# Planned transfer times, ranks and tile counts in a depthwise-attention and selective-scan kernel

## The chip, the cores and the metric

The kernel runs on one core of a Trainium2 chip. Its time is device microseconds of one execution. Five engines take part: TensorE (PE in the profile; its weight loads are listed apart as PEld), VectorE (DVE), ScalarE (ACT), GpSimd (POOL), and SyncE (SP), which here only issues transfers. Each engine runs its own list of instructions in order; semaphores hold an instruction back until what it needs is there.

## The reference

x has 8 images of 56 x 56 positions and 192 channels. Two layers follow each other, both added to x. The first is an attention whose queries and keys come from depthwise 3 x 3 convolutions. The second is a selective scan in four directions. Cut to what matters here:

```python
x = x + conv_attention(group_norm(x))            # layer 0
xz = einsum('bhwc,oc->bhwo', group_norm(x), in_proj_w);  xa, z = split(xz)
xc = silu(depthwise_conv3x3(xa) + conv_b)        # 384 channels
xs = four orders of xc: rows, columns, and both reversed      # L = 3136 positions
dts, Bs, Cs = split(einsum('bkdl,kcd->bkcl', xs, x_proj_weight))
delta = softplus(dt_projs(dts) + dt_projs_bias)
for l in range(L):                               # per direction, 384 channels x 16 states
    h = exp(delta[l] * A) * h + delta[l] * Bs[l] * xs[l]
    y[l] = sum over the 16 states of h * Cs[l]
y = sum of the four directions back in place + xs * Ds
out = x + out_proj(layer_norm(y) * silu(z))
```

## The kernel before, in words

All is done in fp32. The *front* of an image (norms, convolutions, attention, projections; `front` and `x_proj`) writes its results to DRAM. The *scan* then goes through 224 chunks: 8 images x 4 directions x 7 chunks of T = 448 positions. In a chunk the 384 channels lie as 3 blocks (j) of 128 partitions, and there are 16 states n. So there are 3584 pairs (chunk i, state n). The front of the next image and the finish of the last one are done during the scan.

For one chunk, `prepared` loads three tiles (dts, the row inputs of delta; ct, the factors C; du, the scan's input xs), computes delta into dl by a chain PE (L1066), ACT (L1069, L1071), DVE (L1073), ACT (L1078), DVE (L1081), ACT (L1083), DVE (L1085), three times, and lets POOL multiply du by dl (L1089). Then for each n:

- `row_loads` loads row n of B, spread over 128 partitions, into a tile bb (224 KB; a ring of 3 tiles). For the states that POOL sums it also loads the row of C into cb.
- `inputs_made`: POOL makes h = du x bb (L1126; 128 x 1344). The tiles h form a ring of HBUFS = 8.
- `decays`: ACT makes da = exp(dl x A) in PSUM, 3 instructions (L1140), two banks.
- `scans`: DVE scans h in place, 3 instructions (L1157). `carries` keeps the last column (L1179).
- For 11 of the 16 states (13 in the last image), `turned` transposes h on PE (L1203), `scaled` multiplies by C on ACT (L1219), and `back` transposes into the PSUM tile y, summing there (L1237).
- For the other states, `by_pool` multiplies h by cb on POOL (L1256) and adds to yp, one tile (L1260); `summed` adds yp to y on PE (L1275).

When a chunk's y is complete, `evicted` adds it to yacc on DVE (L1290, L1292). `skips` loads xs into yacc before the first direction.

The order in which all this stands on the engines is made by a planner in the kernel itself, `Sched`, when the program is built. Every piece of work is a generator that yields (engine, cost, cells read, cells written). The planner keeps its own clock for each engine, with fixed costs (`t_act`, `t_dve`, `t_pool`). Each time it takes the piece with the least `t - rank`, where t is when the piece could start: a larger rank goes earlier. A transfer yields SP, a cost of 0.07 and a fifth number, the time until its data are there. Cells (`Cell`) hold the planned times of the last write and the last read; a piece cannot start before the cells that it reads are written and those that it writes are no longer read. Ring tiles are given out when they are free in the plan.

`pace` holds the front within 12 us of PE time of a target; when it falls behind, its rank becomes URGENT. `ending` does so for the finish. Where the plan leaves PE idle for over 0.45 us, warm-up matmuls on zeros fill the gap (`keep_busy`, L1371).

The plan decides only the order. On the chip the semaphores decide the time: a planned wait is not executed, but what stands later in an engine's list cannot pass what stands earlier. SP's list is one queue for all transfers: a load that waits for its tile holds all later ones back.

Of the kernel before, what the change touches and what calls it, by code (L numbers as in the profile page):

```python
# [21 lines left out]
T = 448  # L22
# [14 lines left out]
R = 12  # L37
# [4 lines left out]
BY_POOL = (((2, 7), (12,)), ((2, 5), (8, 10), (13,)))  # L42
EPS = 1e-5
CAP = 60.0
HBUFS = 8
LEAD = 3


# [5 lines left out]
PE, ACT, DVE, POOL, SP = range(5)  # L54
LATE = (0.17, 0.08, 0.09, 0.06, 0.0)
HOP = 0.04
URGENT = 0.4


FILL = 64  # L60
# [103 lines left out]
class Sched:  # L164
# [37 lines left out]
    def give(self, s, t):  # L202

        e, cost, reads, writes = s.req[:4]
        end = t + cost
        self.at[e] = end
        self.used[e] += cost
        if s.group is not None and e == PE:
            self.spent[s.group] = self.spent.get(s.group, 0.0) + cost
        end = t + s.req[4] if len(s.req) > 4 else end + LATE[e]  # L210
        for c in reads:
            c.r = max(c.r, end)
        for c in writes:
            c.w = end
        s.end = max(s.end, end)
        self.resume(s)

    def run(self, until=None):
        while True:
# [20 lines left out]
            for s in self.stages:  # L240
# [3 lines left out]
                if s.group in self.limit:  # L244
# [4 lines left out]
                    if spent < must:  # L249
                        rank = URGENT  # L250
                e, _, reads, writes = s.req[:4]
# [21 lines left out]
def kernel(  # L273
# [93 lines left out]
    for nm, src in (("q", bn_q), ("kv", bn_kv)):  # L367
        p = load(f"bn{nm}", [CP, 4, NB], src.rearrange("v (b p) -> p v b", p=CP))
        s = const.tile([CP, NB], F32, name=f"bns{nm}")
        t = const.tile([CP, NB], F32, name=f"bnt{nm}")  # L370
# [30 lines left out]
    s3 = Rings(ctx.enter_context(tc.tile_pool(name="s3", bufs=3)), 3)  # L401
    sh = Rings(ctx.enter_context(tc.tile_pool(name="sh", bufs=HBUFS)), HBUFS)
    c1 = Rings(ctx.enter_context(tc.tile_pool(name="c1", bufs=1)), 1)
# [3 lines left out]
    sc = Sched()  # L407
# [57 lines left out]
    def dma(reads, writes, late, dst, src, after=()):  # L465
        yield SP, 0.07, reads, writes, late
        nc.sync.dma_start(dst, src)
        for t in after:
            t.free()
# [563 lines left out]
    for i in range(2):  # L1033
        t = keep.tile([128, T], F32, name=f"dts{i}")
# [70 lines left out]
    def row_loads():  # L1105
        for i, n in todo:
            b, k, c, _ = steps[i]
            yield lambda: i in chunks
            m = made[b]
            cols = slice(c * T, (c + 1) * T)  # L1110
            bb = yield s3("bb", [128, T])
            yield from dma([m["k_rows"][k, c]], bb.c, 3.2, bb.ap, m["rows"][k][R + n, cols].partition_broadcast(128))
            brow[i, n] = bb
            if n in by[i]:
                cbr = yield s2("cb", [128, T])
                yield from dma([m["k_rows"][k, c]], cbr.c, 3.2, cbr.ap,
                               m["rows"][k][R + NST + n, cols].partition_broadcast(128))
                crow[i, n] = cbr
# [178 lines left out]
    with tc.manual_schedule():  # L1297
        order = [(lay, c) for lay in range(2) for c in range(NCH)]

        with tc.tile_pool(name="p8", bufs=8, space=PSUM) as p8:  # L1300
            banks[0] = Ring(lambda: p8.tile([128, 512], F32, name="bank0"), 8)
            sc.spawn(front(0), 0.0, "front")
            sc.run()
            main = sc.spent.pop("front")
            sc.spawn(x_proj(0, order[:LEAD]), 0.0, "front")
            sc.run()
            each = sc.spent.pop("front") / LEAD

        with ExitStack() as es:
            py = es.enter_context(tc.tile_pool(name="py", bufs=1, space=PSUM))  # L1310
            pa = es.enter_context(tc.tile_pool(name="pa", bufs=2, space=PSUM))
            pb = [es.enter_context(tc.tile_pool(name=f"pb{i}", bufs=1, space=PSUM)) for i in range(3)]
            ybanks = py.tile([128, NJ, 512], F32, name="y")
            nc.vector.memset(ybanks, 0.0)
            ry = Ring(lambda: ybanks, 1)
            rda = Ring(lambda: pa.tile([128, 512], F32, name="da"), 2)
            three = [Tile(1) for _ in pb]

            def share(name, most):
                return Share(three, [lambda p=p: p.tile([128, 512], F32, name=name, tag="bank") for p in pb], most)  # L1320

            rht, rprep = share("ht", 2), share("prep", 1)
            banks[0] = share("bank1", 1)
            at["chunk"] = 0

            for rank, g in enumerate((prepared, skips, row_loads, inputs_made, decays, scans, carries, turned, scaled,
                                      by_pool, back, summed, evicted)):
                sc.spawn(g(), 0.3 + 0.01 * rank, "scan")

            per = NDIR * NCH * NST  # L1330

            def ended(b):
                first = b * NDIR * NCH + (NDIR - 1) * NCH
                yield lambda: at["chunk"] >= first
                yield from finish(b, lambda c: lambda: at["chunk"] >= first + NCH - c, yread[b])

            def arounds():
                for b in range(nb):
                    yread[b] = {}
                    sc.spawn(ended(b), 0.0, "finish")  # L1340
                    if b > 0:
                        yield lambda: at["chunk"] >= b * NDIR * NCH
                    else:
                        yield from sc.join([sc.spawn(x_proj(0, order[LEAD:]), 0.0, "front")])
                    if b + 1 < nb:
                        yield from sc.join([sc.spawn(front(b + 1), 0.0, "front")])
                        yield from sc.join([sc.spawn(x_proj(b + 1, order), 0.0, "front")])

            def pace():

                b, slot = divmod(at["scan"], per)
                whole = main + len(order) * each
                lead = each * (len(order) - LEAD)
                before = b * whole + (lead if b else 0.0)
                here = whole + (0.0 if b else lead)
                late, share = (NDIR - 1) * NCH * NST, 0.87
                part = share * slot / late if slot < late else share + (1.0 - share) * (slot - late) / (per - 2 * NST - late)
                want = before + here * part
                return want + 12.0, want - 12.0

            def ending():
                done = sum(len(r) for r in yread.values())
                b, c = divmod(at["chunk"], NDIR * NCH)
                come = b * NCH + max(c - (NDIR - 1) * NCH, 0)
                return 1e9, 1e9 if done < come - 1 or done < b * NCH else 0.0

            def warm():

                while True:
                    yield PE, T_FILL, [], []  # L1370
                    nc.tensor.matmul(ybanks[:, 0, T:T + FILL], zeros, zeros[:, :FILL], start=False, stop=False)  # L1371

            def may():
                y = ys.get(at["y"])
                return y is not None and y["left"][0] > 0 and y["on"]

            at["y"] = -1
            filler = Stage(warm(), 0.0, 0.0, None)
            sc.resume(filler)
            sc.filler = filler, may  # L1380
            sc.limit["front"] = pace
            sc.limit["finish"] = ending
            sc.spawn(arounds(), 0.0)
            sc.run()
# [58 lines left out]
```

## Time and profile before

| | |
|---|---|
| median of 3 runs | 18865.54 us (18856.12 to 18895.47) |
| the profiled execution | 18891.11 us, span 18889.4 us |
| mean granted clock of TensorE | 0.971 |
| DVE, ACT busy | 14534.5 us, 14643.6 us |
| POOL busy | 16416.5 us |
| PE busy, of it L1371 | 16973.1 us, 1651.3 us |
| DMA | 1750.79 MB, mean 93 GB/s, 32.2% of 16 engines' span |
| L1157 DVE scans | 9216 of mean 1136 ns, 1536 of mean 1077 ns |
| L1126 POOL h | 3584, mean 3050 ns |
| L1089 POOL du | 224, mean 3047 ns |

The profile is of one execution. A row of a group gives busy time, the mean of one instruction and the engine's idle time just before them, with what ended it. A row of waits gives the engine and line that waited, what released it, the total in us, how often, and the longest. In a row in order of time, start and length stand first, and the idle time before it and its releaser in brackets.

### The profile page before, as it was taken

The numbers are of one execution on the slowest core, as the hardware profiler recorded it, in microseconds if no ns is written. First come the engines' busy times: TensorE is split into PE (matmuls) and PEld (weight loads), VectorE is DVE, ScalarE is ACT, GpSimd is POOL, SyncE is SP. The second block draws the span as 40 slices with busy tenths as digits, with TensorE's granted clock in tenths as the row PEclk, the third lists the DMA queues.
The fourth block names the chain that finished last, engine by engine and source line by source line (L and its number), as shares of the span: only waits on it lengthen the run. The fifth ranks groups of instructions, "written<-read, shape, count | busy, mean of one in ns | idle before, by whom it ended". The sixth has DMA issues, their size and how long they took to land. (4 is left out here: it accounts for less than half of the span.)

```text
span 18889.4 us, 274433 instructions
## 1 busy us (share of the span) xinstructions
PE 16973.1 (90%) x96640; PEld 11599.8 (61%) x96640; DVE 14534.5 (77%) x19156; ACT 14643.6 (78%) x26598; POOL 16416.5 (87%) x7528
## 2 busy tenths in 40 slices
PE   8789998999889998899898998889988899988888
PEld 4465566666666656665666655666556665666776
DVE  2387877887778777787777877778777788778887
ACT  2378877787777878778787887878778788888888
POOL 0388998899989999899998999989999899999997
PEclk9899999999999999999999999999999999999999
DMA  1332334323333333322333333332333333342222
GB/s 52 111 89 82 96 96 120 82 85 92 104 112 84 83 95 104 112 84 81 105 100 107 83 84 101 104 106 83 83 96 110 100 83 86 100 120 76 78 78 64
DMA packets 1128347, 1750.79 MB, mean 93 GB/s; under 512 B 168516, under 2 KB 1110840, under 8 KB 1123896
## 3 DMA queue, kind: packets, MB, share of 16 engines
q1 hardware_dynamic: 1126968, 1733.23, 32.2%
q8 instruction: 764, 12.52, 0.3%
q14 instruction: 615, 5.04, 0.1%
HBM read 1545.05 MB, written 187.74 MB: 92 GB/s over the span
## 5 line engine op out<-in xcount | busy, mean ns | idle before, releaser
L1157 DVE TENSOR_TENSOR_SCAN h<-da,newc,h 128x448 f32<-128x448 f32 x9216 | 10111.4, 1136 | 2166.1 <-ACT da L1140 1155.7
L1126 POOL TENSOR_TENSOR h<-du_s,bb 128x1344 f32<-128x1344 f32 x3584 | 10836.0, 3050 | 280.5 <-DMA bb<-rows 246.0
L1140 ACT ACTIVATE da<-dl_s,acoef 128x448 f32<-128x448 f32 x10752 | 6762.2, 636 | 1149.4 <-DVE h L1157 968.0
L1219 ACT ACTIVATE g<-ht,ct_s 112x384 f32<-112x384 f32 x10080 | 5663.7, 576 | 1776.0 <-PE ht L1203 1701.2
L1237 PE MATMUL y<-ident,g 112*128 112x112 f32 x30240 | 4742.3, 271 | 660.2 <-ACT g L1219 506.3
L1237 PEld LDWEIGHTS y<-ident,g 112*128 112x128 f32 x30240 | 3305.9, 143 | 3236.8 <-ACT g L1219 2466.3
L1203 PE MATMUL ht<-ident,h 128*112 128x128 f32 x30240 | 4935.7, 277 | 287.4 <-DVE h L1157 87.4
L1203 PEld LDWEIGHTS ht<-ident,h 128*112 128x112 f32 x30240 | 3481.3, 135 | 1064.4 <-issue 450.9
L1256 POOL TENSOR_TENSOR yp<-h,cb 128x448 f32<-128x448 f32 x1932 | 2147.0, 1143 | 454.8 <-PE y L1275 216.6
L1157 DVE TENSOR_TENSOR_SCAN h<-da,h 128x448 f32<-128x448 f32 x1536 | 1598.9, 1077 | 406.0 <-ACT da L1140 214.3
L1089 POOL TENSOR_TENSOR du_s<-dl_s,du_s 128x1344 f32<-128x1344 f32 x224 | 682.6, 3047 | 1338.5 <-DVE dl_s L1085 1300.8
L1256 POOL TENSOR_TENSOR h<-h,cb 128x448 f32<-128x448 f32 x1260 | 1399.1, 1141 | 291.3 <-issue 175.6
L1371 PE MATMUL y<-zeros 128*128 128x64 f32 x11944 | 1651.3, 272 | 0.0
L1371 PEld LDWEIGHTS y<-zeros 128*128 128x128 f32 x11944 | 1586.1, 198 | 48.6 <-issue 48.6
L1275 PE MATMUL y<-yp,ident 128*128 128x448 f32 x3864 | 1594.0, 547 | 5.1 <-POOL yp L1260 4.5
L453 PE MATMUL bank<-xa,dg 128*128 128x440 f32 (+2 forms) x3024 | 1318.4, 543 | 89.0 <-ACT g L1219 52.2
L1260 POOL TENSOR_TENSOR yp<-yp,h 128x1344 f32<-128x1344 f32 x420 | 1280.9, 3050 | 1.6
L757 PE MATMUL bank<-qT,kT 128*112 128x448 f32 x2352 | 1101.8, 559 | 83.8 <-ACT pT L707 47.2
L766 PE MATMUL bank<-pT,vt 112*128 112x448 f32 x2352 | 1002.1, 546 | 66.8 <-ACT pT L707 43.4
L1275 PEld LDWEIGHTS y<-yp,ident 128*128 128x128 f32 x3864 | 701.3, 193 | 551.6 <-issue 505.2
L453 PE MATMUL bank<-band,dgq 96*96 96x440 f32 (+3 forms) x2016 | 860.9, 544 | 54.4 <-ACT hq L583 29.9
L707 ACT ACTIVATE pT<-bank,nsh 112x448 f32<-112x448 f32 x1176 | 744.3, 635 | 172.9 <-PE bank L757 152.5
(152 smaller groups left out, 12958.1 us busy)
## 6 DMA issues: line engine op xcount, KB each, us to landing
bb<-rows SPq DMA_DIRECT2D x3584, 224.0 KB
cb<-rows SPq DMA_DIRECT2D x1064, 224.0 KB
xt<-x1d SPq DMA_DIRECT2D x224, 336.0 KB
du_s<-xch SPq DMA_DIRECT2D x112, 672.0 KB
du_s<-xcw SPq DMA_DIRECT2D x112, 672.0 KB
xch<-xv SPq DMA_DIRECT2D x24, 1568.0 KB
xcw<-xw SPq DMA_DIRECT2D x168, 224.0 KB
xs<-xch SPq DMA_DIRECT2D x56, 672.0 KB
```

What stands on the lines that cost most here:

```text
L453: nc.tensor.matmul(out[:, o0:o1, a:b], lhs, img(lo, hi)[:, :, a + dx - 1:b + dx - 1], start=(t == TAPS[0]), stop=(t == TAPS[-1]))
L757: nc.tensor.matmul(ps.ap[:TP, :T], kts[h][:, kb * TP:(kb + 1) * TP], qh.ap, start=True, stop=True)
L1126: nc.gpsimd.tensor_tensor(h.ap, du.ap, bb.ap.unsqueeze(1).to_broadcast([128, NJ, T]), ALU.mult)
L1140: nc.scalar.activation(da.ap[:, :T], dl.ap[:, j], AF.Exp, scale=acoef[:, k * NJ + j, n:n + 1])
L1157: nc.vector.tensor_tensor_scan(h.ap[:, j, rev], da.ap[:, 0:T][:, rev], h.ap[:, j, rev], news[i - 1].ap[:, j, n:n + 1] if ci else 0.0, ALU. ...
L1203: nc.tensor.transpose(ht.ap[:TP, j * 128:(j + 1) * 128], h.ap[:, j, s * TP:(s + 1) * TP], ident)
L1219: nc.scalar.activation(g.ap, ht.ap[:TP, :DIN], AF.Copy, scale=ct.ap[:, s, n:n + 1])
L1237: nc.tensor.matmul(y["t"].ap[:, j, s * TP:(s + 1) * TP], g.ap[:, j * 128:(j + 1) * 128], ident[:TP, :TP], is_transpose=True, start=(n == 0 ...
L1256: nc.gpsimd.tensor_tensor(to.ap[:, j], h.ap[:, j], cbr.ap, ALU.mult)
L1260: nc.gpsimd.tensor_tensor(yp.ap, yp.ap, h.ap, ALU.add)
L1275: nc.tensor.matmul(y["t"].ap[:, j, :T], ident, yp.ap[:, j], start=False, stop=(y["left"][j] == 0))
L1371: nc.tensor.matmul(ybanks[:, 0, T:T + FILL], zeros, zeros[:, :FILL], start=False, stop=False)
```

## The change

Five things change, all in what the planner is told. The transfers' planned times grow by MARGIN = 3 us. URGENT rises from 0.4 to 0.9. The ring of bb has 5 tiles, and a load of bb may be planned only AFTER = 2 us past the planned last use of its tile. The ring of h has 7 tiles. And the thirteen generators of the scan get ranks of their own, instead of 0.30 to 0.42 in steps of 0.01 in this order: `prepared` 0.30, `skips` 0.31, `row_loads` 0.32, `inputs_made` 0.33, `decays` 0.34, `scans` 0.35, `carries` 0.36, `turned` 0.37, `scaled` 0.38, `by_pool` 0.39, `back` 0.40, `summed` 0.41, `evicted` 0.42. A tile h takes 5376 bytes of a partition, a tile bb 1792.

```diff
-HBUFS = 8
+HBUFS = 7
...
-URGENT = 0.4
+MARGIN = 3.0
+AFTER = 2.0
+URGENT = 0.9
...
-        end = t + s.req[4] if len(s.req) > 4 else end + LATE[e]
+        end = t + s.req[4] + MARGIN if len(s.req) > 4 else end + LATE[e]
...
-            bb = yield s3("bb", [128, T])
-            yield from dma([m["k_rows"][k, c]], bb.c, 3.2, bb.ap, m["rows"][k][R + n, cols].partition_broadcast(128))
+            bb = yield s3("bb", [128, T], 5)
+            free = Cell()
+            free.w = bb.last() + AFTER
+            yield from dma([m["k_rows"][k, c], free], bb.c, 3.2, bb.ap, m["rows"][k][R + n, cols].partition_broadcast(128))
...
-            for rank, g in enumerate((prepared, skips, row_loads, inputs_made, decays, scans, carries, turned, scaled,
-                                      by_pool, back, summed, evicted)):
-                sc.spawn(g(), 0.3 + 0.01 * rank, "scan")
+            for g, rank in ((prepared, 0.3), (skips, 0.0), (row_loads, 0.25), (inputs_made, 0.0), (decays, 0.37),
+                            (scans, 0.16), (carries, 0.36), (turned, 0.37), (scaled, 0.38), (by_pool, 0.39),
+                            (back, 0.4), (summed, 0.0), (evicted, 0.71)):
+                sc.spawn(g(), rank, "scan")
```

## The prediction

> **What bounds the kernel now.** First the busy times of the page, then the whole kernel cut into start-up (front of batch 0), batches 0 to 6, and the last batch (columns: us, PE, PEld, DVE, ACT, POOL busy with counts, clock, DMA share, GB/s).
>
> ```profile
> PE 16973.1 (90%) x96640; PEld 11599.8 (61%) x96640; DVE 14534.5 (77%) x19156; ACT 14643.6 (78%) x26598; POOL 16416.5 (87%) x7528
> 0.00:786.60 786.60, 645.81 (x1906) 332.98 (x1906) 124.48 (x289) 204.02 (x319) 9.14 (x18) 0.92 0.23 71
> 786.60:16871.00 16084.40, 14559.60 (x82350) 9863.62 (x82351) 12706.36 (x16679) 12698.64 (x23050) 14590.75 (x6746) 0.97 0.34 96
> 16871.00:18889.40 2018.40, 1767.72 (x12386) 1403.21 (x12383) 1703.67 (x2189) 1740.94 (x3229) 1816.60 (x764) 0.96 0.27 78
> ```
>
> PE's 90% contains 1651.3 us of warm-up matmuls (L1371), so it really needs 81%. After start-up POOL is the fullest: 14590.75 of 16084.40 us, 91%, then 90%; DVE and ACT have 79% in the long stage. POOL idles 1494 + 202 us there. Next, who ends POOL's idle time, and SP's (us in total, times, longest):
>
> ```profile
> POOL du_s L1089 <- DVE dl_s L1085: 1300.8, 78, 729.9
> POOL h L1126 <- DMA bb<-rows: 246.0, 74, 9.7
> POOL yp L1256 <- PE y L1275: 216.6, 55, 12.9
> POOL h L1256 <- issue: 175.6, 55, 14.7
> POOL yp L1256 <- issue: 138.0, 75, 5.7
> SPq L467 <- POOL h L1126: 9514.5, 2843, 23.7
> ```
>
> Without the one start-up wait of 729.9 us the first row is 571 us; with what other releasers add, all idle time ahead of L1089 is 608 us after start-up. It is one repeated bubble, the hand-over between chunks. One of them, in order of time:
>
> ```profile
> 8446.12 0.62 DVE L1085 TENSOR_TENSOR dl_s<-prep,dl_s 128x448 f32<-128x448 f32 x1 [1.27 <-ACT prep L1083]
> 8446.82 3.04 POOL L1089 TENSOR_TENSOR du_s<-dl_s,du_s 128x1344 f32<-128x1344 f32 x1 [6.43 <-DVE dl_s L1085]
> 8449.94 9.06 POOL L1126 TENSOR_TENSOR h<-du_s,bb 128x1344 f32<-128x1344 f32 x3
> 8453.02 2.19 DVE L1157 TENSOR_TENSOR_SCAN h<-da,newc,h 128x448 f32<-128x448 f32 x2 [6.28 <-POOL h L1126]
> ```
>
> DVE finishes delta of the next chunk only when it has scanned everything of this one. POOL stands 6.43 us, then needs 3.04 us (du) and 3 us (first h), and DVE stands 6.28 us. I counted on each engine how many scans stand on DVE behind the last delta operation of the next chunk. At 89 of 223 boundaries it is none; there POOL's gap at L1089 averages 6.81 us (606 us, practically all of it). With one it is 0.07 us (33 boundaries), with two or more zero.
>
> **What the Trainium skill says.** "Perfetto Trace Analysis", Identifying the Most-Contended Engine and Optimization Strategy: occupancy is a fair measure for GpSimd, and the gaps on the fullest engine within a regime are what to trace. The numbers above are that reading, and agree. "DMA: Bandwidth & Descriptors", Queues, rings and completion order: on each DMA engine the descriptors of a ring are taken in order. The trace agrees: at 757 us a 21 KB load of dts stands behind seven 672 KB loads of yacc, and PE waits 17.64 us for it. "SBUF — State Buffer", Who interferes with whom: a DVE copy in a two-port mode and GpSimd block each other for a whole instruction. The trace agrees: the 96x2 copy of L430 has a median of 2.44 us and a longest of 9.20 us, beside unbroken POOL work.
>
> **The change, part by part.** No arithmetic is added or removed; the counts of the built programs are equal except warm-up matmuls. What moves is the order.
>
> Ranks. The multiply by inputs (inputs_made) falls from 0.33 to 0 and prepared stays at 0.30, scans fall from 0.35 to 0.16. In the old program L1089 stands directly ahead of its own chunk's first h in all 224 cases. In the new one it stands 2 to 10 h ahead in 223. On DVE, 3 to 13 scans of the old chunk (8 on average) remain when delta is done; none is left at a chunk boundary only for the first chunk. So the bubble goes. What can remain is POOL reaching the earlier du before delta: the h made ahead, less the scans that delta stands behind, is 0 in 7 cases, 1 in 47, more in 170. POOL was 2.1 h ahead of the scans on average, so the 47 may cost up to a scan set of 3 x 1.136 = 3.4 us, 160 us; by the old row 3 us. I take 50, and 7 x 6.81 = 50: 608 - 100 = **508 us gained** (bounds 400 and 608).
>
> bb from 3 to 5 tiles, 3 us margin on every transfer, 2 us behind the release. All are decisions of the planner; no instruction waits longer on the chip by itself. 3 tiles let bb be loaded while two h (6.1 us) are made, and the chain shows landings of 6.57 to 7.10 us; 5 tiles give four h, 12.2 us, less 2. Of the 246 us I keep 50: **196 gained** (bounds 100 and 246). SP's row of 9514.5 us tells that its queue stands on bb's release; behind it stand dts, ct, du and all loads of the front, now issued earlier relative to bb, which is also what feeds delta in time. At start-up the seven yacc loads (skips, rank 0) move behind dts, ct and du: **17 gained** of the 17.64 (0 to 20).
>
> h from 8 to 7 tiles. Nothing waits for an h tile now (1.5 us). With the release times of this trace, the seventh tile back would have been late at 178 h, by 561 us together; much of that would be eaten by slack, as POOL is ahead then. I take **100 lost** (0 to 561).
>
> summed at rank 0 and evicted at 0.71. On PE the sums of yp now stand 1.3 h behind the group's last turned h, against 1.8 ahead; the next write of yp stays 3 or more h away (6.6 on average, was 8.8). The row of 216.6 us can grow: **60 lost** (-50 to 217). Evicting first on DVE is 0.6 us each, hidden by the scans' wait for ACT (1369.9 us); nothing taken; the bound is the 90.5 us that DVE stands before its evictions now (L1290 and L1292), either way.
>
> Longer unbroken POOL runs hold DVE's port longer: DVE's excess over its medians is 160 us now; **40 lost** (0 to 160). URGENT 0.9 only reorders front work inside the same pace window; 0, hidden by the 19% that PE has over; without that cover the 0.5 us between the two ranks at each of 224 chunks, 112 either way. Warm-up matmuls grow from 5972 to 6468, two records each of 138 ns: 137 us of PE, only where the plan leaves PE idle; 0, at most 137.
>
> Sum: -508 - 196 - 17 + 100 + 60 + 40 = -521. The profiled execution, 18891.1 us (span 18889.4), becomes 18370; the median of the runs, 18865.5, stands 25.6 lower: **18345 us**, 2.8% faster.
>
> **Rivals.** (1) The gain goes into the ACT-DVE loop. DVE waits 1369.9 us for da and ACT 968.0 for the scan, with two da banks. Boundaries with one scan of lead have no POOL gap, but their chunks take 82.8 us against 84.4: 89 x 1.6 = 142, and a quarter of bb, 60: about 18665. Against it: three scans of lead have 74.0 us, though these chunks may carry less front work. (2) More goes: POOL's 741 us ahead of L1256 halve too, because by_pool now has 2.9 h made ahead, not 2.2. -608 - 246 - 370 - 17 + 150: about 17775. Against it: those gaps hardly depend on that number now (0.81, 0.72, 0.48, 1.15 us for 1 to 4). (3) Slower: the h ring binds. If POOL must be as far ahead as the earlier du makes it, each release counts as later: shifted by 3 us, 386 h are late by 1410 us together, and with half of it eaten by slack 18865 - 721 + 100 + 705 is 18949. It decides from 621 us on. Against it: 8 tiles were all alive at only 26 of 3584 h. (4) No effect: the orders slip against the real durations until the same bubble stands elsewhere; about 18865. Against it: a lead of 8 scans is 27 us.
>
> **Numbers.** My forecast (18,100 to 18,600) 0.52; rival 1 (18,600 to 18,820) 0.20; rival 2 (17,700 to 18,100) 0.12; rival 3 (18,905 to 19,300) 0.11; rival 4 (18,830 to 18,900) 0.05. The range leaves out rivals 3 and 4 and the lowest third of rival 2: 17,900 to 18,820. Faster or slower means by over 0.2%, about what a measurement of this kernel can tell from no change: 0.84 faster, 0.05 same, 0.11 slower.
>
> **What would show it.** Right: idle ahead of the du multiply after start-up near 100 us, the bb wait under 60, POOL at 93 to 94% of the middle stage, the first du near 769 us. Rival 1: those gone, but DVE's wait for da or ACT's for ht much longer. Rival 3: POOL's L1126 row ended by ht on PE, hundreds of us. Wrong altogether if POOL's idle time stays at 1.7 ms with new names.

## The result, and the profile after

The changed kernel takes 18710.28 us (median of 4 runs, 18697.01 to 18724.76). The kernel before, run beside it, takes 18874.99 us. The ratio is 0.9909, with an interval of 0.9895 to 0.9924: 0.9% faster, 165 us. The forecast was 2.8%, 521 us. So the direction was right and the time lies in the wide range (17,900 to 18,820), but less than a third of the gain came, and it lies outside the forecast's own range (18,100 to 18,600), in that of rival 1.

The profiled execution has a span of 18702.4 us. First the busy times of its page.

```profile
PE 17028.2 (91%) x97632; PEld 11660.0 (62%) x97632; DVE 14685.1 (79%) x19156; ACT 14645.0 (78%) x26598; POOL 16432.2 (88%) x7528
```

No engine works less. DVE is even 151 us busier, to which a section below returns. Next the same cut as before into images 0 to 6, with a front beside the scan, and the last image, without one (columns: us, busy PE, PEld, DVE, ACT, POOL with counts, clock, DMA share, GB/s).

```profile
785.00:16766.50 15981.50, 14620.35 (x82814) 9918.99 (x82814) 12832.52 (x16681) 12713.67 (x23056) 14603.79 (x6746) 0.98 0.34 96
...
16766.50:18702.40 1935.90, 1764.21 (x12909) 1409.86 (x12909) 1728.18 (x2187) 1727.15 (x3224) 1819.25 (x765) 0.99 0.28 80
```

The long stage became 102.90 us shorter (16084.40 before), and the last image 82.50 us (2018.40 before). That is the first finding: the last image, an eighth of the work, brought almost half of the gain. It gained 4.1%, each earlier image 0.6%. Whatever took the gain away sits where a front runs.

Now POOL's waits, and those of its queue of transfers (in us, times, longest).

```profile
POOL du_s L1091 <- DVE dl_s L1087: 881.2, 88, 728.1
POOL h L1260 <- issue: 318.5, 65, 13.9
POOL h L1260 <- DVE newc L1183: 272.9, 131, 12.1
POOL yp L1260 <- PE y L1279: 191.9, 95, 7.6
POOL h L1130 <- PE ht L1207: 190.2, 63, 9.1
POOL h L1130 <- DMA bb<-rows: 110.1, 30, 6.5
...
SPq L469 <- POOL h L1130: 4917.7, 1537, 14.4
SPq L469 <- POOL yp L1260: 3821.5, 419, 30.7
```

The prediction shows the rows of before that go with these, but for one:

```profile
POOL h L1256 <- DVE newc L1179: 93.0, 36, 10.1
```

The lines have moved by 2 to 4: L1089 is L1091 now, L1126 is L1130, L1256 is L1260. The wait for delta was 571.0 us without its start-up part and is 881.2 - 728.1 = 153.1. The wait for bb fell from 246.0 to 110.1, that of SP on bb's release from 9514.5 to 4917.7 us. So far the prediction. But SP's queue now stands at another ring instead: its waits on L1260, which are for the tiles of C's rows (cb), went from 928.1 + 838.9 to 3821.5 + 1765.1 us, so that the three rows together lose only 777 of 11281.5 us. And the h ring makes POOL wait 190.2 us for PE's transposes.

The second products of L1260 (tile h) wait 272.9 us for the carry by name, with 93.0 before. Their rows of "issue", in which the profile names no releaser, belong to the carry as well: all 55 such waits before (175.6 us) and 64 of the 65 now (310.6 of 318.5 us) end 133 ns, as the median, after the end of a carry. So the second products stand some 583 us for the carry now, and some 269 before. All idle time of POOL after the first du went from 1684 to 1482 us, by 202: at the du multiply from 608 to 204 (-404), at L1260's first products (tile yp) from 453 to 281 (-172), at L1260's second products from 288 to 597 (+309), at the h multiply from 262 to 315 (+53). POOL's bubble at the hand-over went, and three quarters of it came back at another line.

A sum helps with all that follows. POOL is busy 16416 to 16440 us in every one of the 20 kernels of this document, and span less POOL's idle time after the first du is 17,205 to 17,229 us in each. So a kernel's time here is a constant plus POOL's whole idle time. That is an account, not a cause; but it says that a wait removed at one line of POOL counts only if the total falls.

### The profile page after: what moved, and what is told of

The parts are those of the page before. It is cut to its first block, busy times and chain, and to the rows that moved or that the text cites. A ratio compares the mean times of both kernels' runs of the same rounds, so it can differ in the third digit from the quotient of the medians.

```text
span 18702.4 us, 276064 instructions
## 1 busy us (share of the span) xinstructions
PE 17028.2 (91%) x97632; PEld 11660.0 (62%) x97632; DVE 14685.1 (79%) x19156; ACT 14645.0 (78%) x26598; POOL 16432.2 (88%) x7528
## 5 line engine op out<-in xcount | busy, mean ns | idle before, releaser
L1130 POOL TENSOR_TENSOR h<-du_s,bb 128x1344 f32<-128x1344 f32 x3584 | 10820.3, 3056 | 321.0 <-PE ht L1207 190.2
L1223 ACT ACTIVATE g<-ht,ct_s 112x384 f32<-112x384 f32 x10080 | 5537.6, 576 | 1170.8 <-PE ht L1207 1046.6
L1241 PE MATMUL y<-ident,g 112*128 112x112 f32 x30240 | 4578.9, 269 | 507.8 <-ACT g L1223 330.5
L1207 PE MATMUL ht<-ident,h 128*112 128x128 f32 x30240 | 4707.2, 275 | 153.3 <-DVE oT L722 52.1
L1207 PEld LDWEIGHTS ht<-ident,h 128*112 128x112 f32 x30240 | 3439.3, 135 | 766.3 <-issue 293.1
L1260 POOL TENSOR_TENSOR yp<-h,cb 128x448 f32<-128x448 f32 x1932 | 2150.8, 1148 | 284.2 <-PE y L1279 191.9
L1260 POOL TENSOR_TENSOR h<-h,cb 128x448 f32<-128x448 f32 x1260 | 1400.7, 1144 | 600.5 <-issue 318.5
L1375 PEld LDWEIGHTS y<-zeros 128*128 128x128 f32 x12936 | 1722.1, 202 | 91.9 <-issue 91.9
L1375 PE MATMUL y<-zeros 128*128 128x64 f32 x12936 | 1773.3, 277 | 0.0
L1279 PE MATMUL y<-yp,ident 128*128 128x448 f32 x3864 | 1742.6, 543 | 8.1 <-POOL yp L1260 5.1
L1091 POOL TENSOR_TENSOR du_s<-dl_s,du_s 128x1344 f32<-128x1344 f32 x224 | 682.5, 3047 | 931.9 <-DVE dl_s L1087 881.2
L455 PE MATMUL bank<-xa,dg 128*128 128x440 f32 (+2 forms) x3024 | 1259.1, 535 | 45.7 <-ACT g L1223 17.9
L709 ACT ACTIVATE pT<-bank,nsh 112x448 f32<-112x448 f32 x1176 | 741.9, 633 | 294.8 <-PE bank L759 236.2
L1068 PE MATMUL prep<-dts,dtw 128*128 128x448 f32 x1344 | 653.1, 568 | 142.7 <-DVE dl_s L1087 130.5
```

Source lines behind the costliest of these rows:

```text
L455: nc.tensor.matmul(out[:, o0:o1, a:b], lhs, img(lo, hi)[:, :, a + dx - 1:b + dx - 1], start=(t == TAPS[0]), stop=(t == TAPS[-1]))
L1130: nc.gpsimd.tensor_tensor(h.ap, du.ap, bb.ap.unsqueeze(1).to_broadcast([128, NJ, T]), ALU.mult)
L1207: nc.tensor.transpose(ht.ap[:TP, j * 128:(j + 1) * 128], h.ap[:, j, s * TP:(s + 1) * TP], ident)
L1223: nc.scalar.activation(g.ap, ht.ap[:TP, :DIN], AF.Copy, scale=ct.ap[:, s, n:n + 1])
L1241: nc.tensor.matmul(y["t"].ap[:, j, s * TP:(s + 1) * TP], g.ap[:, j * 128:(j + 1) * 128], ident[:TP, :TP], is_transpose=True, start=(n == 0 ...
L1260: nc.gpsimd.tensor_tensor(to.ap[:, j], h.ap[:, j], cbr.ap, ALU.mult)
```

## The experiments

Each kernel was run beside the kernel before on the same chip; the medians of the latter lie between 18862 and 18878 us. "Ranks" means the thirteen new ranks of the change.

### The ranks against the rest

The first four kernels split the change: one rank alone, all ranks alone, the rest alone, and the whole with the scans' old rank.

r1_inputs_only, against the kernel before:

```diff
-                sc.spawn(g(), 0.3 + 0.01 * rank, "scan")
+                sc.spawn(g(), 0.0 if g is inputs_made else 0.3 + 0.01 * rank, "scan")
```

> The kernel before with one edit: the rank of inputs_made 0 instead of 0.33. Theory A (the ranks cure the hand-over, and this rank alone is what does it; the idle time then moves to other waits of POOL because DVE sets the pace): POOL's idle time ahead of the du multiply falls from 608 us to about 200, the time to 18,700 to 18,790. Theory B (the gain comes from the transfers: bb's five tiles and the planned margin): 18,850 to 18,890, and the idle time ahead of du stays over 450 us.

Measured: 19027.17 us, ratio 1.0079 (1.0062 to 1.0096), slower by 153. The bubble at the hand-over grew:

```profile
POOL du_s L1089 <- DVE dl_s L1085: 1552.1, 123, 724.0
```

Without the start-up part this is 828 us, 571 before. Delta stands on DVE 1.85 sets of scans ahead of its chunk on average (1.6 before; a set is three scans), and at 96 boundaries none is left behind it (89 before). That the rank of inputs_made alone makes the cure is refuted: delta hardly comes earlier, and POOL stands longer for it.

r2_ranks_only, against the kernel before: the ranks, all else unchanged.

```diff
-                sc.spawn(g(), 0.3 + 0.01 * rank, "scan")
+            for g, rank in ((prepared, 0.3), (skips, 0.0), (row_loads, 0.25), (inputs_made, 0.0), (decays, 0.37),
+                            (scans, 0.16), (carries, 0.36), (turned, 0.37), (scaled, 0.38), (by_pool, 0.39),
+                            (back, 0.4), (summed, 0.0), (evicted, 0.71)):
+                sc.spawn(g(), rank, "scan")
```

> The kernel before with all thirteen new ranks and nothing else. Theory A: nearly all of the gain, 18,710 to 18,780; idle ahead of du about 200 us, the bb wait still about 240. Theory B: 18,830 or more. Theory C (the new ranks lose where the tiles and margins win; a low rank of the scans costs): slower than the kernel before, 18,900 to 19,000.

Measured: 18467.02 us, ratio 0.9781 (0.9767 to 0.9796): **407 us faster than before, and 243 us faster than the whole change**. Its waits:

```profile
DVE h L1157 <- ACT da L1140: 1176.5, 1552, 8.6
...
ACT g L1219 <- PE ht L1203: 974.7, 1245, 11.6
POOL du_s L1089 <- DVE dl_s L1085: 811.8, 50, 724.5
...
POOL yp L1256 <- PE y L1275: 354.9, 99, 33.7
...
POOL h L1256 <- DVE newc L1179: 170.5, 60, 8.8
...
ACT pT L707 <- PE bank L757: 107.6, 150, 15.8
```

The wait for delta is 811.8 - 724.5 = 87.3 us past the start-up. Delta now stands 7.6 sets of scans ahead. POOL's idle time is 1233 us, 451 less than before, for 407 us of time: what went at du did not come back at other lines of POOL. Most of the gain is in images 0 to 6, 355 us from the first h to the last image's; the last image takes 1882 us from its first h to its last scan, as in the whole change (1885; before 1961). So the whole change's loss against this kernel is all in the images with a front.

r3_rest_only, against the kernel after: the old ranks, all else as in the change.

```diff
-            for g, rank in ((prepared, 0.3), (skips, 0.0), (row_loads, 0.25), (inputs_made, 0.0), (decays, 0.37),
...
+            for rank, g in enumerate((prepared, skips, row_loads, inputs_made, decays, scans, carries, turned, scaled,
+                                      by_pool, back, summed, evicted)):
+                sc.spawn(g(), 0.3 + 0.01 * rank, "scan")
```

> The changed kernel with the old ranks: margin, delay behind the release, bb 5, h 7 and URGENT 0.9 remain. Theory A: 18,780 to 18,890, idle ahead of du 450 us or more, the bb wait near 100. Theory B: 18,700 to 18,760. Theory C: faster than the changed kernel, under 18,690.

Measured: 19094.11 us, ratio 1.0115 (1.0100 to 1.0130): 220 us slower than before. The rest alone costs 220 on the old ranks, and 243 on the new ones.

r4_scans_back, against the kernel after:

```diff
-                            (scans, 0.16), (carries, 0.36), (turned, 0.37), (scaled, 0.38), (by_pool, 0.39),
+                            (scans, 0.35), (carries, 0.36), (turned, 0.37), (scaled, 0.38), (by_pool, 0.39),
```

> The changed kernel with the scans' rank back at 0.35. In the changed kernel the carry has 0.20 more than the scans and stands directly behind its own scan, where it starts 2 ns after the scan's end; before it started 55 ns ahead of the end of the instruction before it. Theory A with DVE as the pace (the gain was lost to DVE): the carries overlap again, DVE is busy some 200 us less, POOL's wait at state 5 (454 us) falls by 150 or more, 18,550 to 18,660. Theory D (DVE does not set the pace; the wait at state 5 comes from the h ring or from PE): within 40 of 18,710, or slower because delta comes later again.

Measured: 18945.84 us, ratio 1.0036 (1.0023 to 1.0049), 236 us slower than the change. Delta's lead falls from 7.6 sets of scans to 2.7, and 41 boundaries have none. It is the scans' fall from 0.35 to 0.16, below the 0.30 of `prepared`, that brings delta early: DVE is where delta ends, so what must yield is the work that competes with it on DVE. The time, though, isn't lost at the hand-over:

```profile
POOL yp L1260 <- PE y L1279: 573.9, 121, 17.8
```

POOL waits 187 us for delta past the start-up (915.7 - 729.0), only 34 more than in the change, but 573.9 us for PE's sums of yp, with 191.9 in the change. So the lead is shown to come from the scans' rank; that the 236 us come from the lead is not.

### Which part of the rest takes the gain back

From the kernel after, one part undone at a time: the ring of bb (with its delay), the margin, URGENT.

```diff
r6_bb3:
-AFTER = 2.0
+AFTER = 0.0
...
-            bb = yield s3("bb", [128, T], 5)
+            bb = yield s3("bb", [128, T])
r7_no_margin:
-MARGIN = 3.0
+MARGIN = 0.0
r8_urgent:
-URGENT = 0.9
+URGENT = 0.4
```

> The changed kernel with three tiles bb and no delay behind the release; margin, h 7, URGENT 0.9 and the ranks remain. Theory B (two more tiles and the delay cost, because row loads run ahead and block SP's queue on the tiles of C): 18,470 to 18,600. The forecast (they gain by the bb wait): 18,780 to 18,900, with a bb wait of 200 us or more. Theory U, M or H: within 60 of 18,710.

> The changed kernel with MARGIN 0. Theory M: 18,470 to 18,560. Theory U, H or B: within 60 of 18,710.

> The changed kernel with URGENT back at 0.4. The ranks alone gave 18,467; the rest of the change takes about 245 us back, all of it in images 0 to 6, where front work runs. Theory U (URGENT at 0.9 lets late front work go ahead of ready scan work on every engine): 18,470 to 18,560. Theory M (the planned margin does it): within 60 of 18,710. Theory H (the h ring of 7) and theory B (bb's ring and delay): also within 60 of 18,710.

Measured, as ratios to before: r6_bb3 18771.07 us, 0.9952 (0.9937 to 0.9967); r7_no_margin 18746.50 us, 0.9938 (0.9922 to 0.9953); r8_urgent 18567.82 us, 0.9844 (0.9829 to 0.9858). Taking the tiles and the delay away costs 61 us, the margin 36, but taking URGENT 0.9 away **gains 142 us**, more than half of the 243 that the change loses against the ranks alone. I had costed it at nothing. The other way round, from the ranks alone:

r9_ranks_urgent and r10_ranks_h7, each r2_ranks_only with one line more:

```diff
r9_ranks_urgent:
-URGENT = 0.4
+URGENT = 0.9
r10_ranks_h7:
-HBUFS = 8
+HBUFS = 7
```

> The kernel before with the new ranks and URGENT 0.9. The counterpart of putting URGENT back: theory U says that 0.9 costs whatever else is changed, so 18,570 to 18,680, with PE's idle time ahead of front matmuls in images 0 to 6 up from 305 us to 400 or more. If URGENT hurts only together with the margin (theory UM): 18,440 to 18,510.

> The kernel before with the new ranks and 7 tiles h. Theory H: 18,600 or more, and POOL waits for ht on PE at its h multiply some 150 us longer than with 8. Theory U, M or B: 18,440 to 18,510. The forecast had 100 us for this ring.

Measured: r9_ranks_urgent 18779.85 us, 0.9953 (0.9938 to 0.9967), which is 313 us slower than the ranks alone. r10_ranks_h7 18465.45 us, 0.9789 (0.9772 to 0.9805): the seventh tile costs nothing, although POOL now waits 155.9 us for PE's transposes. The waits of r9_ranks_urgent, to be read against those of r2_ranks_only:

```profile
DVE h L1157 <- ACT da L1140: 1399.1, 1804, 8.5
ACT g L1219 <- PE ht L1203: 1149.4, 1518, 17.9
...
POOL du_s L1089 <- DVE dl_s L1085: 767.5, 30, 725.0
...
POOL h L1256 <- DVE newc L1179: 375.2, 73, 17.7
ACT pT L707 <- PE bank L757: 353.1, 253, 28.6
```

The hand-over is better than ever here: 42.5 us for delta past the start-up. Still the kernel loses 313 us. The row that says most is the last: ACT stands before the attention's exponential (L707) for its score matmul (L757), 353.1 us, where it stood 107.6. DVE waits 222.6 us more for da from ACT, and POOL 204.7 us more for the carry from DVE. ACT's wait for the scan's transposes on PE grew too, by 174.7 us, so L707 need not be the only place. A stretch of the same kernel in order of time (start, length; in brackets the idle time before and its releaser):

```profile
6094.39 0.63 ACT L1140 ACTIVATE da<-dl_s,acoef 128x448 f32<-128x448 f32 x1
...
6094.55 1.42 PE L757 MATMUL bank<-qT,kT 128*112 128x448 f32 x2
...
6095.05 1.15 DVE L1157 TENSOR_TENSOR_SCAN h<-da,newc,h 128x448 f32<-128x448 f32 x1 [0.65 <-ACT da L1140]
...
6096.00 0.64 ACT L707 ACTIVATE pT<-bank,nsh 112x448 f32<-112x448 f32 x1 [0.98 <-PE bank L757]
6096.53 1.19 ACT L1140 ACTIVATE da<-dl_s,acoef 128x448 f32<-128x448 f32 x2
...
6097.20 1.15 DVE L1157 TENSOR_TENSOR_SCAN h<-da,newc,h 128x448 f32<-128x448 f32 x1 [1.00 <-ACT da L1140]
```

ACT finishes one da at 6095.02 and has to begin L707, because it stands next in its list; PE is not through with the scores. ACT stands 0.98 us. Only behind L707 come the next da, so DVE, done at 6096.20, stands 1.00 us. POOL is busy throughout this stretch, so it shows how such a stand arises, not what it costs. I read URGENT at 0.9 so: in the plan it lets an operation of the late front go ahead of a decay that could run at once, and an engine that takes its list in order then stands. PE's own idle time ahead of front matmuls in images 0 to 6 (L501 to L852, without the lines that norms and convolutions share) fits: 305 us with the ranks alone, 488 with URGENT 0.9; 447 in the whole change, 260 in it with URGENT 0.4. So does ACT's wait for the scores: 236.2 us in the change, 110.9 in it with URGENT 0.4. POOL's idle time, however, moves differently between these two: URGENT 0.9 adds 231 us at the second products, 156 at the h multiply and 72 at du, and takes 316 off at the first products. So that URGENT costs is shown in both settings; the chain by which it costs is read from one stretch and from the waits of r9_ranks_urgent.

Two more kernels narrow it, r17_urgent_06 with 0.6 in place of 0.9, and r19_urgent_evict, with 0.9 and `evicted` raised from 0.71 to 1.01, above the urgent front, as 0.71 is with 0.4:

```diff
r17_urgent_06 (the ranks, and):
-URGENT = 0.4
+URGENT = 0.6
r19_urgent_evict (the ranks, and):
-URGENT = 0.4
+URGENT = 0.9
-                            (back, 0.4), (summed, 0.0), (evicted, 0.71)):
+                            (back, 0.4), (summed, 0.0), (evicted, 1.01)):
```

> Ranks and URGENT 0.6. If late front work costs in proportion to how far it goes ahead of the scan (0.4 gave 18,467, 0.9 gave 18,780): 18,540 to 18,640, with PE's idle time ahead of front matmuls between 305 and 488 us. If only standing above evicted (0.71) or another threshold counts: within 40 of 18,467.

> Ranks with the eviction at 1.01 instead of 0.71, and URGENT 0.9. If the cost of 0.9 comes from late front work going ahead of the eviction of y: 18,450 to 18,550. If it comes from going ahead of the scan's transposes, products and decays by more than half a microsecond: 18,720 to 18,840.

Measured: r17_urgent_06 18479.21 us, 0.9787 (0.9773 to 0.9802), 12 us from the ranks alone, and ACT's wait at L707 is 128.8 us. r19_urgent_evict 18694.65 us, 0.9907 (0.9888 to 0.9927), still 228 us above the ranks alone, with 357.9 us at L707. So the harm lies between 0.6 and 0.9, and passing the eviction is at most the smaller part (85 us). Rank counts in us of the plan: 0.9 lets the front go ahead of decays (0.37) that could start up to 0.53 us earlier, 0.6 up to 0.23. That 0.53 is about a score matmul (562 ns) fits, but is argued, not shown.

All kernels with the new ranks together (without r4_scans_back and r14_ranks_carry, which move a rank back) fall into two groups. The ten with URGENT 0.4 or 0.6 take 18465 to 18662 us, and ACT stands 106 to 137 us at that line; the five with 0.9 take 18695 to 18780 us, and ACT stands 162 to 358 us. Within the second group the wait doesn't order the times: r6_bb3 has 162 us and is the second slowest. The granted clock orders nothing: it is 0.971 to 0.983 in these kernels, with 0.979 in r6_bb3 and 0.974 in r10_ranks_h7, which is 306 us faster.

### The transfers

The prediction gave the five tiles 196 us. One kernel starts from the ranks alone (r12), the others from r10_ranks_h7, since the change has 5 tiles bb beside 7 tiles h:

```diff
r12_ranks_margin (the ranks, and):
-        end = t + s.req[4] if len(s.req) > 4 else end + LATE[e]
+        end = t + s.req[4] + 3.0 if len(s.req) > 4 else end + LATE[e]
r13_ranks_bb5 (the ranks, HBUFS = 7, 5 tiles bb, delay of 2 us):
-            bb = yield s3("bb", [128, T])
-            yield from dma([m["k_rows"][k, c]], bb.c, 3.2, bb.ap, ...
+            bb = yield s3("bb", [128, T], 5)
+            free = Cell()
+            free.w = bb.last() + 2.0
+            yield from dma([m["k_rows"][k, c], free], bb.c, 3.2, bb.ap, ...
r15_bb5_no_after (the ranks, HBUFS = 7, 5 tiles bb): no delay
r16_bb3_after (the ranks, HBUFS = 7, delay of 2 us): 3 tiles bb
```

> The kernel before with the new ranks and the margin of 3 us on all planned transfers. With URGENT at 0.4, tiles and margin together left 100 us (18,568 against 18,467). If it is the margin: 18,530 to 18,620. If it is bb's ring and delay: 18,440 to 18,500. If neither alone: 18,440 to 18,520 in both runs.

> The kernel before with the new ranks, 7 tiles h, 5 tiles bb and the delay of 2 us; no margin, URGENT 0.4. If bb's ring and delay cost: 18,530 to 18,620. If they gain what the forecast had (the 200 us for which POOL waits for bb with 7 tiles h and 3 tiles bb): 18,250 to 18,350. If the bb wait is covered by other waits: 18,420 to 18,500 with a bb wait under 60 us.

> Ranks, 7 tiles h, 5 tiles bb, no delay behind the release. If the delay is what costs: 18,430 to 18,510. If the two tiles cost (row loads run ahead and stand on SP for the tiles of C, so that other loads come late): 18,600 to 18,700. If neither is a cause by itself but any new order costs or gains 100: anywhere between 18,440 and 18,650.

> Ranks, 7 tiles h, 3 tiles bb, planned 2 us behind the release. If the delay costs (three tiles are two h of 3.05 us ahead, and 2 us of that are gone): 18,600 or more and a bb wait above 250 us. If the tiles cost and not the delay: 18,440 to 18,510.

| bb tiles, delay (ranks, 7 h) | us | ratio to before | POOL's wait for bb |
|---|---|---|---|
| 3, none (r10_ranks_h7) | 18465.45 | 0.9789 (0.9772 to 0.9805) | 200.8 |
| 5, none (r15_bb5_no_after) | 18497.70 | 0.9797 (0.9782 to 0.9811) | 74.3 |
| 5, 2 us (r13_ranks_bb5) | 18640.05 | 0.9878 (0.9861 to 0.9894) | 95.7 |
| 3, 2 us (r16_bb3_after) | 18662.37 | 0.9885 (0.9871 to 0.9900) | 394.4 |

The margin on the ranks alone costs 49 us (r12_ranks_margin 18516.16 us, 0.9812, 0.9798 to 0.9827).

Two more tiles do take the wait for bb away, from 200.8 to 74.3 us, and the time does not follow (+32). POOL stands as long elsewhere: its wait for the carry goes from 275.0 to 332.5 us, that for PE's transposes from 155.9 to 193.8. These two took back three quarters of what bb lost (57.5 + 37.9 of 126.5), and POOL's idle time in all went from 1252 to 1276 us. I read it so: POOL is let go earlier to where DVE or PE would have held it anyway. The delay costs 142 us with 5 tiles, 197 with 3. With 3 the wait for bb shows it, 193.6 us more. With 5 tiles it doesn't (95.7 us): POOL's idle time grows by 81 us ahead of the h multiply and by 73 ahead of the first products, and what makes it is open. Now the delay with the margin in place: r20_two_undone is the change with both URGENT and the delay undone, and differs from r8_urgent by the delay alone.

```diff
r20_two_undone (against the kernel after):
-AFTER = 2.0
-URGENT = 0.9
+AFTER = 0.0
+URGENT = 0.4
```

> The changed kernel with URGENT 0.4 and no delay behind the release. If these two parts are what takes the gain back: 18,440 to 18,530. If margin and tiles cost as well when together: 18,550 to 18,600.

Measured: 18552.88 us, 0.9833 (0.9818 to 0.9849). The delay costs 15 us here, against 142 without the margin. Taken the other way, the margin costs 55 us without the delay (r15 to r20) and gains 72 with it (r13 to r8). Why the two go together so is open.

How much does a mere other order change? HOP is a constant of the planner with no part in the change.

```diff
r18_hop (the ranks, and):
-HOP = 0.04
+HOP = 0.045
```

> The new ranks with the planner's constant between two engines 0.045 instead of 0.04 us: a change that means nothing, but gives another order. If single orders scatter little: within 40 us of 18,467. If the scatter is of the size of the smaller effects (margin 49, bb's ring 175): off by 60 to 200, to either side.

Measured: 18502.22 us, 0.9799 (0.9783 to 0.9816), 35 us above the ranks alone. This is one sample of what re-planning does without a reason, and it gives no bound. So of the differences above, the +32 of the tiles, the 36, 49 and 55 of the margin, the 61 of tiles and delay, the 12 of URGENT 0.6, the 15 of the delay and the 85 of the eviction are not read by themselves. 142, 197, 228 and 313 are four times as large or more; for URGENT the two groups above say the same, for the delay with 3 tiles the wait for bb; for the delay with 5 tiles there is no such second sign.

### The carries, an explanation that fell

DVE's extra 151 us I put down to the carries:

```profile
L1179 DVE TENSOR_REDUCE newc<-h 128x3 f32<-128x3 f32 x3584 | 516.6, 144 | 28.4
...
L1183 DVE TENSOR_REDUCE newc<-h 128x3 f32<-128x3 f32 x3584 | 557.3, 156 | 88.7
```

The first row is from before. On average a carry now starts 2.2 ns past its predecessor's end, where it began 54.6 ns before it and was so far covered. That is 56.8 ns x 3584 = 204 us of DVE's time. But no single carry starts at 2.2 ns: the average is of two kinds. Here is one of each in the changed kernel:

```profile
8442.03 2.18 DVE L1161 TENSOR_TENSOR_SCAN h<-da,newc,h 128x448 f32<-128x448 f32 x2
8444.25 0.16 DVE L1183 TENSOR_REDUCE newc<-h 128x3 f32<-128x3 f32 x1
...
8448.66 0.59 DVE L1083 SCALAR_TENSOR_TENSOR dl_s<-prep,dl_s 128x448 f32<-128x448 f32 x1
8449.18 0.14 DVE L1183 TENSOR_REDUCE newc<-h 128x3 f32<-128x3 f32 x1
```

The first stands directly behind its own third scan, whose last column it reads: such a carry starts 34 ns past that scan's end (33 to 36 ns in all of them) and takes 159 ns. The second stands behind other work and starts about 80 ns before that work's end. 2560 of the 3584 are of the first kind now, 804 were before. Before, 1330 stood behind a scan of the next state, of which they read nothing; now none does. I took the 204 us for a reason of the missing gain. r14_ranks_carry gives the carries the scans' rank, so that they part again:

```diff
r14_ranks_carry (the ranks, and):
-                            (scans, 0.16), (carries, 0.36), (turned, 0.37), (scaled, 0.38), (by_pool, 0.39),
+                            (scans, 0.16), (carries, 0.16), (turned, 0.37), (scaled, 0.38), (by_pool, 0.39),
```

> The kernel before with the new ranks, but the carry at 0.16 like the scans, so that it no longer goes directly behind its own scan. Theory A (DVE's time counts): the carry overlaps again, DVE is busy some 200 us less, and the time falls to 18,300 to 18,420. Theory E (DVE has enough over; what counts is how early the carry comes, since POOL's products wait for it): POOL's wait for newc grows, 18,470 to 18,600.

Measured: 19229.31 us, 1.0191 (1.0176 to 1.0207), 762 us slower than the ranks alone.

The carries are back at a mean of 144 ns and begin 59 ns before their predecessors' ends, and DVE is 231 us less busy after the first du. Nothing is won by that. In the waits POOL's stand for delta is back:

```profile
POOL du_s L1089 <- DVE dl_s L1085: 1453.3, 120, 724.7
```

In the order of the lists delta leads as before (7.55 sets of scans), but at the 98 boundaries where POOL stands over 1 us for it, it stands 7.51 us on average, while DVE begins 4.8 scan instructions and is idle for less than 1 us: DVE is behind POOL there, though it has less to do. So the carries' overlap is not what the change lacks, and a lead in the list is not enough by itself. What makes this edit so dear is open. r4_scans_back agrees as far as it goes: only 647 of its carries stand directly behind their own scan, and it was slower too.

## Why the prediction was right or wrong

The parts, each measured on top of the one above it, add up to the result:

| step | us | over the one above | forecast |
|---|---|---|---|
| before | 18874 | | |
| ranks (r2_ranks_only) | 18467.0 | -407 | -508 +60 +40 and -17 at start-up = -425 |
| h 8 to 7 (r10_ranks_h7) | 18465.5 | -2 | +100 |
| bb 3 to 5 (r15_bb5_no_after) | 18497.7 | +32 | together -196 |
| margin (r20_two_undone) | 18552.9 | +55 | |
| delay (r8_urgent) | 18567.8 | +15 | |
| URGENT (the change) | 18710.3 | +142 | 0 |

The -521 and the -165 differ by 356: 298 in the three steps of the transfers, 142 at URGENT, 18 at the ranks, less 102 at the h ring. Two terms therefore failed: the 196 us that the transfers were to gain, and the 0 for URGENT; the 100 us that the h ring did not cost hide a part of both. The split is that of this order; on the ranks alone URGENT costs 313, the margin 49, and tiles and delay 175 (with 7 h), 537 together, more than the 407 gained. With URGENT at 0.9, taking away the margin or the tiles and delay made it slower by 36 and 61 us. The parts don't add up the same in every order, since each re-plans the whole list.

**Ranks: the mechanism held, the size in part by luck.** The prediction named the ranks of inputs_made, prepared and scans together and said that delta would be done some 8 sets of scans before the chunk ends; the trace has 7.6. r1_inputs_only shows that the first of these ranks alone costs 153 us, r4_scans_back that the scans' rank makes the lead, which the prediction didn't separate. With the ranks alone 451 us went at L1089 (608 to 157), not 508, and the 60 and 40 us that were to be lost beside it did not show: idle time ahead of the first products grew by some 10 us, since the wait for PE's sums rose from 216.6 to 354.9 while other waits there fell. So the agreement of -425 with -407 is of errors that offset each other. In the whole change du gave 404 us, and 309 came back at the second products, a wait for the carry that has no term in the prediction's sum.

**URGENT: "only reorders front work inside the same pace window; 0", with "112 either way".** This step failed outright. I counted where work could wait in PE's 19% and did not ask which scan operations stand behind a front operation on ACT, and who waits for them. Measured: 142 us in its place, 313 on the ranks alone, both outside the bound. The chain that the traces suggest is the one above: scores, L707, da, scan, carry, second product. The waits of the kernel before had a row to start from, ACT's wait at L707 for L757, 152.5 us; the prediction doesn't use it.

**bb: "Of the 246 us I keep 50: 196 gained".** This is the largest error of the table: the wait fell (to 110.1), not the time. Tiles, margin and delay cost 102 us together where 196 were to be gained. The step that failed is that a wait removed at one line was counted as time: with the tiles alone 126.5 us less waiting for bb left the time 32 us longer, as POOL stood at the carry and at PE's transposes instead. "No instruction waits longer on the chip by itself" is true and beside the point: a planned wait is not executed, but it changes what is put ahead, and the delay cost 142 us without the margin, 15 with it.

**Start-up: "17 gained".** The first du went from 783.58 to 781.94, the first h from 788.39 to 789.45: nothing gained. The start of the changed kernel in order of time:

```profile
749.31 0.38 SPq L469 DMA_DIRECT2D dts<-rows  x1
...
750.70 6.85 SPq L469 DMA_DIRECT2D yacc<-xch  x7
751.13 0.99 PE L1068 MATMUL prep<-dts,dtw 128*128 128x448 f32 x2 [3.00 <-DMA dts<-rows]
...
757.64 17.42 SPq L469 DMA_DIRECT2D xs<-xch  x3
...
769.69 3.33 PE L916 MATMUL bank<-xs,xpw 128*128 128x448 f32 x4 [17.57 <-DMA xs<-xch]
```

The load of dts does go ahead of yacc, and delta's first matmul waits 3.00 us, not 17.64. But now the loads for x_proj (L916) stand behind the seven of yacc, PE waits 17.57 us for them, and in PE's list delta's next matmuls, at 772.81 us, come after L916. The Trainium skill ("DMA: Bandwidth & Descriptors", Queues, rings and completion order) has the descriptors of a ring taken in order on each DMA engine, and both starts agree, with 17.64 us before and 17.57 us now. The prediction read it rightly for one load; which load stands behind next was not asked.

**Small terms.** The h ring cost -2 for 100: POOL waits 155.9 us for transposes with 7 tiles and 36.2 with 8, and the time stays; that this falls where POOL is ahead, as the prediction had it, isn't shown. The sums of yp on PE were to cost 60: the change's wait is 191.9 us (216.6 before). DVE's excess over its medians was to grow by 40; counted over instructions that take over 50 ns more than the median of their line and tiles, it fell from 154 to 125 us.

**The rivals.** Rival 1 named the number (18,665, range from 18,600) by another cause: it held the ACT-DVE loop for a floor at 18,665, and r2_ranks_only runs 198 us below that. Its signs, a longer wait of DVE for da or of ACT for ht, did not come in the change:

```profile
DVE h L1161 <- ACT da L1144: 1272.9, 1689, 5.8
ACT da L1144 <- DVE h L1161: 1319.4, 2180, 24.3
ACT g L1223 <- PE ht L1207: 1046.6, 1424, 11.3
```

DVE's wait for da was 1369.9 before, ACT's for ht 1701.2; only ACT's wait for the scan grew, from 968.0. Rival 2 (by_pool's gaps halve) met the opposite: they went from 741 to 878 us. Rival 3 (the h ring) is refuted by r10_ranks_h7, rival 4 (the bubble stays under other names) by r2_ranks_only for the ranks; in the whole change three quarters of the bubble did come back elsewhere.

Of all kernels run, the ranks alone, with 8 or 7 tiles h, are the fastest: 2.2% faster than before, 1.3% faster than the change (18467.02 / 18710.28 = 0.987).

## What to carry to other kernels

Where engines take their lists in order, put the work that the next chunk needs ahead of the present chunk's on the engine where that work ends; letting the consumer alone go earlier made it worse here (by 153 us). An urgency that lets late background work pass operations that could start at once can make an engine stand for inputs that aren't there, and the loop behind it, so ask of each engine what stands next after the urgent piece. A wait removed is worth only what the next wait leaves: follow the whole idle time of the fullest engine, not one of its lines. When a planner re-plans everything, run several neutral re-plannings first (one moved the time by 35 us here) to know which differences mean something.

## What the runs showed of the hardware that was not expected

In the changed kernel a 128x3 reduction on DVE that stands directly behind the scan whose output it reads starts 34 ns past that scan's end and takes 159 ns (2560 cases, 33 to 36 ns). In the kernel before, one directly behind a scan of which it reads nothing starts 83 ns before that scan's end and takes 132 ns (1330 cases). So a small operation that depends on its predecessor cost 117 ns more at its start and 27 ns more in its length than one that does not; for 1756 more carries of the first kind the start alone makes an estimated 205 us of DVE, close to the 204 us above.
